# A second level of Strassen's scheme in four of the seven products of Q, K and V

## The chip, the core and the metric

The kernel runs on one core of one Trainium2 chip. The core has a matrix engine (TensorE, PE in the profile; its weight loads are the row PEld), a vector engine (VectorE, DVE), a scalar engine (ScalarE, ACT), a general engine (GpSimd, POOL) and a queue that issues most transfers (SyncE, SP). Each engine works through its own list of instructions in order and waits at semaphores for the others. The metric is device time in microseconds of one execution; the time shown is the median of three runs.

## The reference, cut to what matters

```python
x = L0_attn_a_x                                   # 8 x 512 x 1024, fp32
x = x + _L0_attn_a_ref(_layernorm(x), qkvw, qkvb, ow, ob)
x = x + _L0_ffn_ref(_layernorm(x), weight, bias, centroids, assignments)
x = x + _L0_attn_b_ref(_layernorm(x), bv_q, bv_k, bv_v)
x = x + _L0_ffn_ref(_layernorm(x), weight, bias, centroids, assignments)

def _L0_attn_a_ref(x, attn_qkvw, attn_qkvb, attn_ow, attn_ob):   # 32 heads of 32
    qkv = x @ attn_qkvw + attn_qkvb
    ...
    scores = jnp.einsum('bhqd,bhkd->bhqk', q, k) * scale
    probs = jax.nn.softmax(scores, axis=-1)
    ctx = jnp.einsum('bhqk,bhkd->bhqd', probs, v)
    return ctx @ attn_ow + attn_ob
```

The change concerns the first attention alone: the product `x @ attn_qkvw` (4096 x 1024 by 1024 x 3072) and how its result and the context are kept.

## The kernel before

All work is fp32. The program has four stages one after the other: softmax attention (some 2490 of 3715 us), a gated dense layer, a sigmoid attention, and the dense layer again. The instruction order on each engine is the order in which the Python code records it.

**Units.** The softmax attention runs over `units = 64` units: 8 batches of 512 tokens by `NC = 8` groups of four heads (128 columns of Q, K and V). Unit n is batch n // 8, group n % 8. In its turn unit n does the scores, exponentials and values of its own heads, while the row maxima of unit n + 1 and the projections of unit n + 2 are made beside it.

**The loop over a unit** (`for n in range(units)`, with `for i in range(TPB)` inside, four quarters). Each quarter records, in this order: `rows_step(n + 1, i)`, a block of scores (TensorE, L905) into the four PSUM banks `sc`, and its row maxima `nmax` by one reduction (VectorE, L906); a piece of side work and of the *filler* (`between`); `keys_step(n, i)`, which writes the same four banks again, first with the maxima as a shift (L934), then with the scores (L937), and ScalarE's exponential of them (L939); then more filler. `sum_step` adds the four exponential blocks (one addition by GpSimd in two halves, L948, two by VectorE, L950), `values_step` multiplies them with V (L961), `normalize` divides by the sum (L973 to L982) and writes the context `ctxT`. Quarter 0 also has `turn_max`, a small transposition (`tpm`) that takes its PSUM buffer from the same ring of three (`ps_m`, tag "mm") as all projections.

**The filler** is a queue of TensorE pieces of about 0.9 us each: the projections of unit n + 2 (`project_pieces`) and the out products of an earlier batch (`out_products`, shared over the units by `OUT_SHARES` and `LAST_SHARES`), woven into each other. `between` takes its share of the queue (`FILLER_SHARES`). Side work (`side`) is what VectorE, SP and GpSimd do for later batches: normalizing x (`norm_tasks`), the sums of the left matrices (`left_tasks`), of the weights (`sum_weights`) and of the out weights (`ow_sum_tasks`).

**Projections.** For batch 0 (units 0 to 7) they are plain products (`first_pieces`). From unit 8 on they follow Strassen's scheme in Winograd's form: seven products instead of eight, from sums of the left matrix (`LEFT`: A11, S2, A12, S3, A22, S1, S4) and of the right (`RIGHT`: B11, T2, B21, T3, T4, T1, B22). The left matrix is the normalized x, split in two halves of tokens and two halves of the 1024 inputs. The right matrix of Q and K is one unit's Q columns beside its K columns; that of V is the columns of two units. Each product has 256 tokens, 512 inputs and 128 columns and is gathered into the outputs by VectorE additions straight from PSUM (`gather`, with two ScalarE copies for the first product): L156 and L158. The T sums of the weights are made once in batch 0 and kept in DRAM; a `Stream` of blocks of 256 KB (`W_BUFS = 6` buffers) brings them back for each unit, in the order of `order`. The matmul itself is in `product` (L578), which splits a product by columns into matmuls of width 64 or 32.

**Context and out products.** The context of a whole batch is one tile `ctxT` (two of them in turn, 16 KB per partition each); its out products (again seven instead of eight per pair of token tiles) run during the next batch.

Of the kernel before, what the change touches and what calls it, by code (L numbers as in the profile page):

```python
# [13 lines left out]
F32 = mybir.dt.float32  # L14
# [3 lines left out]
ALU = mybir.AluOpType  # L18
# [19 lines left out]
W_BUFS, OW_BUFS = 6, 6  # L38
FILLER_SHARES = (0.5, 0.5, 0.6, 1.0, 1.0, 1.0, 0.7, 1.0, 1.0)

OUT_SHARES = (2, 2, 2, 1)

OUT_SUMS = {0: (0,), 5: (1, 2), 7: (3,)}
LAST_SHARES = {-7: 0, -6: 1, -5: 1, -4: 2, -3: 2, -2: 6, -1: 2}
# [103 lines left out]

def gather(nc, k, acc, ia, ib, ja, jb, bias=(None, None), early=False):
# [49 lines left out]
class Stream:  # L199
# [6 lines left out]
    def fill(self, upto):  # L206
        while self.loaded < min(upto, len(self.sources)):
            k = self.loaded
            self.tiles[k] = self.pool.tile(self.shape, F32, tag=self.tag, name=f"{self.tag}_{k}")
            self.nc.sync.dma_start(self.tiles[k], self.sources[k]())  # L210
            self.loaded += 1
# [209 lines left out]
def softmax_attention(tc, cst, stage, filler, clusters, pools, dr, late, args):  # L421
# [14 lines left out]
    fixed, ctxp, rpool, npool = outer("a_fixed", 1), outer("a_ctx", 2), outer("a_r", 3), outer("a_n", 1)  # L436
    owpool, csp, xTp, sump = outer("a_ow", OW_BUFS), outer("a_cs", 1), inner("a_xT", 2), inner("a_sum", 1)
    wpool, xpool = inner("a_w", W_BUFS), inner("a_x", 2)
    qkpool, vpool, ptp, tmp = inner("a_qk", 3), inner("a_v", 5), inner("a_pt", 3), inner("a_tmp", 1)
# [9 lines left out]
    xTs, ctxTs, state, lefts = {}, {}, {}, {}  # L449
    units, half = B * NC, NC // 2  # L450

    def quarter(t, g, k):

        return w_view[:, ts(k, half), ts(t * NC + g, P)]

    def weight_source(kind, g, name):

        if name[0] == "T":
            return dr.sums[kind, g, name].rearrange("p (c n) -> p c n", c=half)
        t, g = ((0, g) if name[2] == "1" else (1, g)) if kind == "qk" else (2, 2 * g + int(name[2]) - 1)  # L460
        return quarter(t, g, int(name[1]) - 1)

    V_PARTS = (RIGHT[:4], RIGHT[4:])
    order = []
    for u in range(NC, units):
        g = u % NC
        order += [("qk", g, RIGHT[k]) for k in EARLY] + [("v", g // 2, name) for name in V_PARTS[g % 2]]
# [11 lines left out]
    used, side, tiles, waiting, ready, held = {"w": 0}, deque(), deque(), deque(), deque(), []  # L479

    def first_norm():
# [5 lines left out]
        def load(i):  # L487
            pool, tag = (npool, ("n1", "nT")[i % 2]) if i > 1 else (xpool, "x")
# [31 lines left out]
    def norm_tasks(b):  # L520
# [9 lines left out]
        def load(i):  # L530
            st[i] = xpool.tile([P, H], F32, tag="x", name=f"x_{b}_{i}")
            nc.sync.dma_start(st[i], x[ts(b * TPB + i, P), :])
# [23 lines left out]
        def apply(k, j):  # L556
# [5 lines left out]
            [partial(load, 0), partial(load, 1)],  # L562
            [partial(turned, k) for k in range(NC // 2)] + [partial(stats, 0), partial(stats, 1)],
            [partial(load, 2), partial(load, 3)],
            [idle] * 3 + [partial(stats, 2), partial(stats, 3)],
            [root, shift, send, idle, spread],
            [idle, idle, *scaled[:3]],
            [idle, idle, *scaled[3:6]],
            [idle, idle, *scaled[6:]],
# [10 lines left out]
    first_w = {}  # L580

    def load_first(g, kinds):

        if g >= NC:
            return
        if not first_w:
            first_w["qk"] = ctxp.tile([P, NC, S], F32, tag="ctxT", name="w_first")
        if 2 in kinds:
            wv = rpool.tile([P, H], F32, tag="r", name=f"wv_{g}")
        for t in kinds:  # L590
            for k in range(2):
                at = ts(k, S) if t == 2 else ts((g % 2) * 4 + 2 * t + k, S)
                flat = wv if t == 2 else first_w["qk"].rearrange("p c t -> p (c t)")
                w = first_w[t, g, k] = flat[:, at].rearrange("p (c n) -> p c n", c=half)
                nc.sync.dma_start(w, quarter(t, g, k))
# [1129 lines left out]
```

## Time and profile before

| what | value |
|---|---|
| median of three runs | 3717.14 us (3715.69 to 3718.55) |
| span of the profiled execution | 3715.1 us |
| instructions | 76365 |
| GpSimd busy | 594.9 us, 16% |
| mean granted TensorE clock | 0.999 |
| bytes moved, mean rate | 598.55 MB, 161 GB/s |
| L906, reduction of scores, VectorE, x256 | 586.0 us, 2289 ns each |
| L950, sums of exponentials, VectorE, x128 | 292.0 us, 2281 ns each |
| L158, gather with bias, 128x256, x224 | 107.6 us, 480 ns each |
| L156, gather, 128x256 (v and qk), x196 and x168 | 79.8 and 70.0 us, 419 and 417 ns each |
| L578, matmuls of Q and K after batch 0 (128x256) | 408.5, 202.0, 119.2 and 19.5 us |
| L578, matmuls of V after batch 0 (128x128) | 198.4, 162.5 and 19.7 us |

How to read it: "busy" is the time in which an engine executes; a line like `128*64 128x256 f32 x16` is a group of 16 matmuls that contract 128 rows, use 64 columns of the array and move 256 columns. Each fp32 matmul of the program shows as two records. In brackets at the end of a timeline row stands how long the engine was idle before it and what ended that. Between the span and the median lie 2 us.

### The profile page before, as it was taken

How to read it: one execution, taken by the hardware profiler on the slowest of the kernel's cores; microseconds unless marked ns; L12 is line 12 of the kernel's file. 1: busy time of each engine (PE TensorE's matmuls, PEld its weight loads, DVE VectorE, ACT ScalarE, POOL GpSimd, SP SyncE). 2: the span in 40 equal slices, each digit the busy share in tenths (PEclk: the TensorE clock that was granted, in tenths of full speed). 3: DMA queues.
4: the chain of work that ended last, by engine and by line, in shares of the span. 5: the costliest groups of instructions: out<-in, count | busy, mean ns of one | idle time of the engine just before them, and what ended most of it. 6: DMA issues, size and time to landing. Idle time of an engine off the chain costs nothing.

```text
span 3715.1 us, 76365 instructions
## 1 busy us (share of the span) xinstructions
PE 3677.4 (99%) x32792; PEld 1876.7 (51%) x32792; DVE 2539.7 (68%) x3497; ACT 927.8 (25%) x1017; POOL 594.9 (16%) x574
## 2 busy tenths in 40 slices
PE   8999999999999999999999999999999999999999
PEld 4444544544545455445445445444444467774444
DVE  4777676767667677766767767666788845556656
ACT  1222222222222222222222222222111144430000
POOL 1222111111111111111111111111000044530000
PEclk9999999999999999999999999999999999999999
DMA  5335444645655555465465454347566767763332
GB/s 184 113 122 179 142 143 147 192 138 157 185 153 150 159 162 163 133 198 152 139 182 159 143 150 124 122 156 244 158 180 179 184 186 234 222 220 127 133 132 98
DMA packets 728641, 598.55 MB, mean 161 GB/s; under 512 B 322152, under 2 KB 574064, under 8 KB 728304
## 3 DMA queue, kind: packets, MB, share of 16 engines
q1 hardware_dynamic: 701072, 496.40, 46.6%
q0 software_dynamic: 22912, 81.54, 5.7%
q10 hardware_dynamic: 4320, 15.73, 1.0%
q8 instruction: 259, 4.24, 0.5%
q14 instruction: 78, 0.64, 0.0%
HBM read 459.30 MB, written 134.25 MB: 160 GB/s over the span
## 4 chain that ended last, share of the span: by engine, by line
PE 95%; DVE 3%; DMA 1%; issue 1%; ACT 0%; POOL 0%; SPq 0%; DVEq 0%; ACTq 0%; POOLq 0%
PE mm L578 42%; PE dense L1285 20%; PE sc L905 7%; PE av L961 6%; PE sc L937 6%; PE csc L1347 4%; PE o L1366 4%; PE sc L934 2%; PE logitsT L339 1%; PE den L973 1%; PE tp L291 1%; DVE nmax L906 1%; DVE sum L950 1%; PE tpm L578 0%; DVE s L1377 0%
## 5 line engine op out<-in xcount | busy, mean ns | idle before, releaser
L906 DVE TENSOR_REDUCE nmax<-sc 128x4 f32<-128x2048 f32 x256 | 586.0, 2289 | 295.3 <-PE sc L905 295.2
L939 ACT ACTIVATE pT<-sc 128x2048 f32<-128x2048 f32 x256 | 480.8, 1878 | 1122.3 <-PE sc L937 1122.3
L948 POOL TENSOR_TENSOR sum<-pT,pT 128x1024 f32<-128x1024 f32 x128 | 309.4, 2438 | 750.0 <-ACT pT L939 678.1
L578 PE MATMUL mm<-xT,w 128*64 128x256 f32 (+1 forms) x3736 | 428.1, 383 | 0.0
L578 PEld LDWEIGHTS mm<-xT,w 128*64 128x64 f32 (+1 forms) x3736 | 241.5, 135 | 204.1 <-issue 54.3
L578 PE MATMUL mm<-s,w 128*32 128x256 f32 (+1 forms) x3672 | 321.2, 381 | 1.2 <-DVE qk L158 1.2
L950 DVE TENSOR_TENSOR sum<-sum,pT 128x2048 f32<-128x2048 f32 x128 | 292.0, 2281 | 0.9 <-ACT pT L939 0.9
L905 PE MATMUL sc<-qk,qk 32*64 32x512 f32 x4096 | 285.1, 613 | 0.5 <-ACT pT L939 0.4
L156 DVE TENSOR_TENSOR u<-dense,u 128x512 f32<-128x512 f32 x223 | 148.0, 685 | 184.7 <-PE dense L1285 169.3
L578 PEld LDWEIGHTS mm<-s,w 128*32 128x32 f32 (+1 forms) x3672 | 180.4, 122 | 180.4 <-issue 68.9
L937 PE MATMUL sc<-qk,qk 32*128 32x512 f32 x2048 | 263.7, 589 | 0.0
L578 PE MATMUL mm<-ow,ctxT 128*32 128x512 f32 (+2 forms) x1276 | 247.2, 599 | 3.0 <-DMA ow<-o_T 2.8
L961 PE MATMUL av<-pT,v 128*32 128x512 f32 x2048 | 246.4, 598 | 0.2 <-ACT pT L939 0.2
L1285 PE MATMUL dense<-sum,s 128*128 128x512 f32 x512 | 231.8, 593 | 0.0
L578 PEld LDWEIGHTS mm<-w,xT 128*64 128x64 f32 (+1 forms) x3888 | 197.5, 133 | 62.2 <-issue 48.9
L578 PE MATMUL mm<-w,xT 128*64 128x128 f32 (+1 forms) x3888 | 218.1, 274 | 0.0
L158 DVE SCALAR_TENSOR_TENSOR qk<-mm,qkvb_s,qk 128x256 f32<-128x256 f32 x224 | 107.6, 480 | 123.2 <-PE mm L578 119.2
L1285 PE MATMUL dense<-wT_s,dT_b 128*128 128x512 f32 x384 | 171.2, 593 | 0.0
L1285 PE MATMUL dense<-wT_s,dT_a 128*128 128x512 f32 x384 | 171.2, 593 | 0.0
L578 PE MATMUL mm<-ow,c 128*64 128x512 f32 (+2 forms) x864 | 169.9, 596 | 0.2 <-DMA ow<-in_ow 0.2
L578 PE MATMUL mm<-w,s 128*64 128x128 f32 x2688 | 162.5, 274 | 0.0
L578 PEld LDWEIGHTS mm<-w,s 128*64 128x64 f32 x2688 | 148.0, 137 | 22.9 <-issue 22.9
(236 smaller groups left out, 4468.8 us busy)
## 6 DMA issues: line engine op xcount, KB each, us to landing
w<-in_qkvw SPq DMA_DIRECT2D x252, 256.0 KB, 3.0
ow<-o_T SPq DMA_DIRECT2D x240, 256.0 KB, 3.6
w<-qk_T SPq DMA_DIRECT2D x224, 256.0 KB, 2.8
ow<-in_ow SPq DMA_DIRECT2D x180, 256.0 KB, 3.3
w<-v_T SPq DMA_DIRECT2D x112, 256.0 KB, 2.7
x<-in_x SPq DMA_DIRECT2D x32, 512.0 KB, 5.3
dT_a<-xT SPq DMA_DIRECT2D x32, 512.0 KB, 5.7
x_a<-x SPq DMA_DIRECT2D x32, 512.0 KB, 6.5
```

What stands on the lines that cost most here:

```text
L156: nc.vector.tensor_tensor(out, acc, other, ALU.add)
L578: nc.tensor.matmul(out[cols], lhsT[:, cols], rhs, **flags)
L905: nc.tensor.matmul(sc[ts(j, P // 2), h, :], st["q"][rows, cols], st["k"][rows, :], start=True, stop=True)
L906: nc.vector.tensor_reduce(st["nmax"][:, qt, :], sc, AX.X, ALU.max, negate=True)
L937: nc.tensor.matmul(sc[:, h, :], st["k"][rows, ts(kt, P)], st["q"][rows, :], start=False, stop=True)
L939: nc.scalar.activation(pT, sc, AF.Exp, scale=SCALE_A)
L948: nc.gpsimd.tensor_tensor(st["sum"][:, h, :], st["pT", 0][:, h, :], st["pT", 1][:, h, :], ALU.add)
L950: nc.vector.tensor_tensor(st["sum"], st["sum"], st["pT", kt], ALU.add)
L961: nc.tensor.matmul(st["av"][rows, :], st["v"][:, kt, rows], pT[:, h, :], start=(kt == 0), stop=(kt == TPB - 1))
L1285: nc.tensor.matmul(st["acc"], st["left"][LEFT[k]][:, c, :], self.w[RIGHT[k]][:, c, :], start=(c == 0), stop=(c == half - 1),)
L1347: nc.tensor.matmul(sc[:, AT_OFF[i] : AT_OFF[i] + n], k[:, c, ts(i, P)], xT[:, c, i * P :], start=(c == 0), stop=(c == 1),)
L1366: nc.tensor.matmul(acc[:, j - jj, :], at[:, start : start + P], self.v[b * TPB + i][:, cols], start=(i == 0), stop=(i == j),)
```

## The change

Of the seven products of Q, K and V, four (S2, A22 and A12, S3 with their right sides) are made by a second Strassen step; the other three (A11 by B11, S1 by T1, S4 by B22) stay as they are. The four are taken in two pairs (`TWICE = ((2, 4), (1, 3))`): the inner products of a pair are summed in one PSUM accumulator of 128x2x128, so that a pair costs seven accumulators with four 128-column products each.

- Projections come in jobs: Q and K for two units (`("qk", n, part)`, two parts, one per unit of the loop), V for four units (`("v", n, part)`, four parts). `parts_of(u)` says which parts unit u carries in its filler.
- Each inner product is gathered by the same seven additions and two copies as an outer one; the three outer products are added by `done`, for two halves of the columns each.
- `left_tasks` makes the inner left sums too, in two portions in groups 4 and 5 of the batch before; `weight_sums` makes the inner weight sums in batch 0 and stores them with GpSimd's queue in `dr.twice` and `dr.once`, spread by `SUM_STEPS`.
- The weight stream now covers batch 0 as well and reads 20 blocks per job.
- The context is kept in six quarter slots (`ctx_s`, `SLOTS`), the last one in a spare tile that `settle` copies at the end of the loop.
- The rows of x for the layer norm are loaded into the place of the later `xT`, earlier than before; `qk` tiles go from 3 to 5, `v` from 5 to 7, out weight buffers from 6 to 5; the out products are shared otherwise.

```diff
-W_BUFS, OW_BUFS = 6, 6
+W_BUFS, OW_BUFS = 6, 5
+QK_BUFS, V_BUFS, SLOTS = 5, 7, 6
+SUM_STEPS = (16, 16, 16, 16, 10, 10, 10, 10, 9)
-OUT_SHARES = (2, 2, 2, 1)
+OUT_SHARES = (1, 2, 2, 2)
-LAST_SHARES = {-7: 0, -6: 1, -5: 1, -4: 2, -3: 2, -2: 6, -1: 2}
+LAST_SHARES = {-7: 0, -6: 0, -5: 1, -4: 2, -3: 4, -2: 4, -1: 3}
+TWICE = ((2, 4), (1, 3))
+STORED = ("B11", "T3", "B21", "B22", "T1", "T2", "T4")
...
+    def parts_of(u):
+        parts = [("first", u + 2, 0)] if u + 2 < NC else []
+        n = u + 3 if u % 2 else u + 2
+        if NC <= n < units:
+            parts.append(("qk", n, 0 if u % 2 else 1))
+        n = u - u % half + half
+        if NC <= n < units:
+            parts.append(("v", n, u % half))
+        return parts
+    def blocks_of(kind, n, part):
...
+        nodes = {"qk": ((0, 1), (2, 3, 4)), "v": ((0,), (1,), (2, 3), (4,))}[kind][part]
...
+        def twice(i, k, at):
+            def go():
+                assert i in left["made"]
+                acc, w = ps_m.tile([P, 2, P], F32, tag="mm", name="mm"), weights.tiles[at]
+                w = w.rearrange("p (a c) n -> p a c n", a=2)
+                for a in range(2):
+                    for c in range(2):
+                        lhsT, rhs = w[:, a, c, :], left[TWICE[i][a]][k][:, c, :]
+                        if not qk:
+                            lhsT, rhs = rhs, lhsT
+                        product(acc[:, a, :], lhsT, rhs, start=(c == 0), stop=(c == 1))
+                if k == 0:
+                    make(i)
+                o = [target(i, j) for j in range(2)]
+                gather(nc, k, acc, *(o[j][:, :, m, :] for m in range(2) for j in range(2)), early=True)
+                weights.done(at)
...
+        def done(node, j, acc):
+            (ia, ja), (ib, jb) = ([target(side, j)[:, m] for m in range(2)] for side in range(2))
+            qb, kb = (bias(side, j) if qk else None for side in range(2))
+            if node == 0:
+                add(ia, acc, qb)
+                add(ib, acc)
+                add(jb, ib)
+                add(ja, jb, qb)
+            elif node == 5:
+                add(jb, acc, kb)
+                add(ib, acc)
+            else:
+                add(ib, acc, kb)
...
+        steps = [
+            partial(tt, e1, b21, b22, ALU.add), partial(tt, e2, e1, b11, ALU.subtract),
+            partial(tt, e3, b11, b21, ALU.subtract), partial(tt, e4, b12, e2, ALU.subtract),
+        ]
+        steps.append(partial(last, 0))
+        steps += [partial(tt, a21, a11, a21, ALU.subtract), partial(tt, s2, a22, a21, ALU.subtract)]
+        more = [partial(tt, s4, a12, s2, ALU.subtract), partial(tt, s1, s2, a11, ALU.add)]
+        for node, t in ((1, s2), (3, a21)):
+            q11, q12, q21, q22 = quarters(t)
+            e = againp.tile([P, 3, 2, P], F32, tag=f"e{node}", name=f"e{node}_{b}")
+            names, own = left_sums(nc, q11, q12, q21, q22, *(e[:, k] for k in range(3)))
+            left[node] = [names[name] for name in LEFT]
+            more += own
+        more.append(partial(last, 1))
+        return steps, [partial(together, more[a:b]) for a, b in ((0, 1), (1, 6), (6, 11))]
...
+    def settle():
+        kept = ctxs[B - 1, 1]
+        first, second = sorted(free_slots[:2])
+        del free_slots[:2]
+        ctxs[B - 1, 1] = ctx_s[:, first : second + 1 : second - first]
+        for m in range(2):
+            nc.scalar.copy(ctxs[B - 1, 1][:, m], kept[:, m])
...
-            if g == NC - 2:
-                side.extendleft(reversed(left_tasks(b + 1)))
-            filler.add(weave(project_pieces(ahead), products), mark=ahead)
+        if b + 1 < B and g in (half, half + 1):
+            if g == half:
+                left_steps = deque(left_tasks(b + 1))
+            side.extendleft(reversed(left_steps.popleft()))
+        pieces = [piece for part in parts_of(n) for piece in job_pieces(*part)]
...
-    nc = bacc.Bacc("TRN2", target_bir_lowering=False, num_devices=1)
+    nc = bacc.Bacc("TRN2", target_bir_lowering=False, num_devices=1, dynamic_dma_scratch_size=4096)
```

## The prediction

> **What bounds the kernel now.** I read the page's busy line first, then the chain of waits, then one whole batch of the attention loop in the windows view, then the few places where TensorE waits at all.
>
> ```profile
> span 3715.1 us, 76365 instructions
> ...
> PE 3677.4 (99%) x32792; PEld 1876.7 (51%) x32792; DVE 2539.7 (68%) x3497; ACT 927.8 (25%) x1017; POOL 594.9 (16%) x574
> ...
> PE 95%; DVE 3%; DMA 1%; issue 1%; ACT 0%; POOL 0%; SPq 0%; DVEq 0%; ACTq 0%; POOLq 0%
> ```
>
> TensorE is never idle for long (38 us in all), so any matmul taken away shortens the run, as long as nobody else becomes late. One steady batch of the loop (eight units, from 1011.1 to 1328.8 us) shows who could:
>
> ```profile
> 1011.10:1328.80 317.70, 317.39 (x3734) 160.17 (x3733) 226.02 (x304) 84.43 (x83) 44.22 (x25) 1.00 0.54 160
> ```
>
> The columns are length, PE, PEld, DVE, ACT, POOL, clock, DMA share and GB/s. VectorE has 317.7 - 226.0 = 91.7 us free per batch. But it works in order, and each score block L905 must be reduced (nmax, L906) before the next block can be written (L934) into the same four PSUM banks. The one place in the loop where VectorE had too much to do shows the price; first TensorE, then VectorE, in order of time:
>
> ```profile
> 287.49 1.11 PE L905 MATMUL sc<-qk,qk 32*64 32x512 f32 x16
> 288.53 1.08 PE L578 MATMUL mm<-s,w 128*64 128x256 f32 x8
> 289.44 1.90 PE L578 MATMUL mm<-xT,w 128*64 128x256 f32 x16
> 293.64 0.41 PE L934 MATMUL sc<-shift,ones_h 32*128 32x512 bf16 x4 [2.30 <-DVE nmax L906]
> ```
>
> ```profile
> 278.86 2.29 DVE L906 TENSOR_REDUCE nmax<-sc 128x4 f32<-128x2048 f32 x1 [0.73 <-PE sc L905]
> 281.06 2.28 DVE L950 TENSOR_TENSOR sum<-sum,pT 128x2048 f32<-128x2048 f32 x1
> 283.26 1.22 DVE L1377 TENSOR_TENSOR s<-xT 128x1024 f32<-128x1024 f32 x1
> ...
> 291.31 2.28 DVE L906 TENSOR_REDUCE nmax<-sc 128x4 f32<-128x2048 f32 x1
> ```
>
> Between two reductions VectorE had 12.45 us of work, TensorE between the score blocks only 9.6. The second reduction started late and TensorE stood 2.30 us. In all, waits of this kind are few:
>
> ```profile
> PE sc L934 <- DVE nmax L906: 4.7, 5, 2.3
> ...
> PE tpm L578 <- DVE parts L916: 1.3, 2, 1.0
> ```
>
> So the kernel is bound by TensorE, with VectorE behind it at a small distance, in quarters of a unit.
>
> **The change, part by part. TensorE.** The six groups of L578 that make Q, K and V after the first batch have 408.5 + 202.0 + 119.2 + 19.5 us (128x256) and 198.4 + 162.5 + 19.7 us (128x128), less a little of other work: about 1130 us. Four of seven products cost 7/8 afterwards: 1/14 less, 81 us at most. I counted it again through the instruction lists of both kernels as built, cut at each score block, with prices from undisturbed stretches of the timeline: a full 128x128 product of 256 columns 0.451 us (1028.44 to 1032.05: eight products), of 128 columns 0.219 (1004.46 to 1006.21: eight), at width 32 0.46 and 0.2475. From the first to the last score block this gives 2423.5 us before and 2348.5 after. The tail of out products left behind grows by 1.0. TensorE: -74 us. The lists show that the change does what it says (84 groups of four 128-column products in each later batch), so that rival is dropped.
>
> [...] The rows show 2 x 0.219 = 0.438 against 0.451, no loss, and I keep 74.
>
> **VectorE.** Per batch the lists have 52 additions of 128x256 out of PSUM before and 136 after, besides 32 scalar_tensor_tensors in both: each inner product needs its own seven additions, then the outer sums 14 more per job. 84 x 0.417 (L156, v and qk) = 35.0 us. Left sums: four of 512 and eight of 256 more, 4 x 0.69 + 8 x 0.417 = 6.1. So +41 us per batch, 226 to 267 us, while TensorE falls from 317.7 to about 307 (the row sums of units 24 to 31 are 313.0 and 302.6). Additions from SBUF to SBUF at 128x256 are not in the trace; the nearest row (L1158, 256 wide) has 0.402, L156 has 0.417; I take 0.417. ScalarE's copies stay 24 per batch at 0.375.
>
> On average that still fits; by quarter it doesn't. Back to back, an operation takes its time less 0.08 us (the reduction 2.29, the next starts after 2.20), and 0.12 more where it needs the one before. Units 24 to 31 (all steady batches are alike), first and last quarter, TensorE / VectorE in us:
>
> | unit | 24 | 25 | 26 | 27 | 28 | 29 | 30 | 31 |
> |---|---|---|---|---|---|---|---|---|
> | first, before | 10.5/9.2 | 11.4/9.2 | 12.3/7.7 | 10.5/10.0 | 10.5/9.2 | 11.4/9.2 | 12.3/11.2 | 10.5/7.5 |
> | first, after | 10.5/12.8 | 11.4/10.7 | 11.4/11.0 | 10.5/12.7 | 10.5/15.1 | 11.4/14.6 | 11.4/11.0 | 10.5/13.0 |
> | last, before | 8.4/8.0 | 8.4/10.3 | 9.2/6.6 | 8.4/10.4 | 8.4/7.9 | 8.4/9.0 | 9.2/6.6 | 8.4/9.0 |
> | last, after | 8.4/8.3 | 8.4/9.5 | 8.6/12.7 | 8.5/8.4 | 8.4/9.6 | 8.4/8.3 | 8.6/11.4 | 8.5/8.0 |
>
> The 15.1 of unit 28, as an example: reduction 2.2, sum of exponentials 2.2, four inner left sums 2.5, two groups of four outer additions 3.4, statistics 1.6, normalizing 2.4, two more additions 0.8. The cover is the filler between a score block and its L934, less 2.35 for the reduction: 3.6 - 2.35 = 1.25, or 0.35 to 0.45 where the filler is 2.7 to 2.8. What VectorE has over TensorE is carried on, and TensorE stands for what exceeds the cover. Unit 28: 15.1 - 10.5 - 1.25 = 3.3. Unit 29: 1.2 carried + 3.2 - 0.4 = 4.0. Unit 27: 4.1 carried from the eight additions at once in unit 26 - 1.4 = 2.8, then 1.35 + 2.2 - 1.25 = 2.2. Unit 31: 1.5 and 2.6 likewise. Unit 24: 1.0. The middle quarters give nothing. Sum 17.4 us per batch.
>
> Over all units: 19.0 in the first batch (weight sums there), 18.7 in the second, 84.4 in the five after it, 9.4 in the last, 131.5 in all. The same count on the kernel before gives 9.6, against 6.0 measured in the two rows above; in the quarter shown it has 12.73 for 12.45. I take 2% off VectorE's times for that: 115 after, 6 before. VectorE: +109 us. Bounds: 4% off and 0.6 us more cover give 79; the raw count 131.5. Behind a standing L934 stand the exponentials (L939), the next score block and everything else in TensorE's order; nothing overtakes.
>
> **Transfers.** Weight blocks after the first batch grow from 588 to 840 of 256 KB, 36 more per batch, 9.4 MB in 307 us: 160 to about 191 GB/s. The page has slices of 234 and 244 GB/s without TensorE waiting, and a block lands 2.9 us after its issue; with six buffers five inner blocks of 4 x 0.219 = 0.88 us cover 4.4 us. I take 0; the ring of ow falls from six to five (5 x 0.9 = 4.5 us against 3.6), and ow waits were 2.8 us before; upper bound 20. The rows of x for the next batch now come four at once and earlier, into the place of the later xT: the same eight transfers on SP, whose queue stands 1524 us behind L578 already (SPq L210); 0. GpSimd issues 108 stores instead of 48 in the first batch at 0.54 + 0.18 us, 43 us beside its 15 to 25% busy there; 0, at worst eight groups of four in front of the sums of exponentials: 8 x 2.9 = 23. **End of the loop:** two copies of 1024 elements by ScalarE stand between the last normalizing and the out products; by its 128x512 rows (0.69) between 1 and 3 us; I take 2.
>
> **Sum:** 3715.1 - 74 + 109 + 2 = 3752 us span. The median is 2 us above the profiled span, so 3754.
>
> **Rivals.** (1) VectorE stays hidden: the additions take slack that really exists (68% busy), and the run falls by the whole TensorE term: 3717 - 74 + 2 = 3645. For it speaks the average, 267 of 307 us; against it the stop of 2.30 us at an excess of 2.85. It decides if fewer than 10 us of stops show on L934. 6%. (2) Stops, but half: if the additions run at 0.34 back to back even in chains and the cover is 0.6 longer, the count with 8% off is 54: 3717 - 74 + 52 + 2 = 3697, faster. Against it the agreement in the steady quarters (11.17 counted, 11.15 measured in unit 30). It turns to slower when stops exceed 80 us. 15%. (3) Weight and ow rings run dry or GpSimd's stores hold VectorE's sums as well: another 20 + 23 on top, about 3797. 7%.
>
> **How the numbers follow.** The forecast case, VectorE's queue takes more than TensorE gives back, holds 72%: 3722 (stops 79) to 3771 (131.5, less 6). The range 3690 to 3800 takes in (2) and (3) and leaves out (1). 0.2% is 7.4 us, about what a measurement of this kernel can tell. Faster: (1) and most of (2), 0.20; the same: the low end of the forecast and the high end of (2), 0.08; slower 0.72.
>
> **What would show it.** Right: L578's Q, K, V groups lose some 75 us; VectorE's busy time grows by about 320 us (7 x 41, and 40 of weight sums: twelve groups of 4 x 0.69 + 8 x 0.417 = 73 after, 48 x 0.69 = 33 before); the row "sc <- DVE nmax" grows from 4.7 to about 100 us, most of it in units 24, 27, 28, 29 and 31 and their like; the span of a steady batch is 307 + 17 = 324 instead of 317.7. Wrong: that row under 40 us, or waits for w or ow above 20, or TensorE's busy time not lower.

## The result, and the profile after

The changed kernel takes 3982.28 us (median of 4 runs, 3977.65 to 3983.76), the kernel before beside it 3716.41 (4 runs): 1.0712 times as long, 95% interval 1.0697 to 1.0728. The forecast was 3754. The direction was right, the size was not: 266 us more instead of 37.

From the page of the kernel after, span, busy time by engine, and the shares of the chain of waits:

```profile
span 3975.9 us, 80821 instructions
...
PE 3687.1 (93%) x34128; PEld 1930.6 (49%) x34128; DVE 2838.2 (71%) x4265; ACT 944.1 (24%) x1047; POOL 647.8 (16%) x634
...
PE 65%; DVE 20%; DMA 6%; issue 5%; SPq 2%; POOL 1%; ACT 0%; DVEq 0%; POOLq 0%; ACTq 0%
```

TensorE has less to do and yet is busy 10 us longer (3677.4 before). Idle it is for 289 us instead of 38. Both are seen in the windows view: batch 0 before, then batch 0 and one steady batch after, each from its first reduction to the first of the next batch (columns: length, busy PE, PEld, DVE, ACT, POOL, clock, DMA share, GB/s):

```profile
42.58:317.00 274.42, 271.47 (x2840) 122.59 (x2842) 186.89 (x204) 70.85 (x58) 62.77 (x67) 0.99 0.39 124
```

```profile
40.24:434.96 394.72, 313.72 (x3288) 152.09 (x3288) 260.18 (x364) 73.19 (x65) 115.73 (x127) 0.91 0.61 183
...
1093.30:1437.68 344.38, 316.07 (x3888) 167.62 (x3888) 260.04 (x394) 86.52 (x87) 43.96 (x25) 0.97 0.58 174
```

Length less busy PE is the idle time: 81 us in batch 0 and 28 in the steady batch, against 3 and 0.3. And the clock is new: 0.91 and 0.97. In the clock's records of the whole run TensorE is at half speed for 182 us, in 38 stretches (8 us in 3 stretches before). A stretch often begins while TensorE still stands, and idle time is not lost twice: busy it is for 135 of the 182 us (6.8 before), and half of that, 64 us more than before, is what the clock cost. What remains of the busy time without that half is the work at full speed: 3674.0 us before and 3619.5 after. So 251 us more idle + 64 of clock - 54 of work = 261, the difference of the two spans. The work is a remainder here, but a steady one: 307.6 to 307.8 us in each of batches 2 to 6 (315.0 to 315.2 before), whatever the clock did there. By stage, before and after (us; half clock is time spent at 0.5, and how much of it TensorE was busy; batch 7 ends at the first reduction of its last unit):

| stage | length | idle | half clock | busy at half clock |
|---|---|---|---|---|
| start | 42.6 to 40.2 | 12.2 to 11.1 | 0 to 3.4 | 0 to 3.4 |
| batch 0 | 274.4 to 394.7 | 2.9 to 81.0 | 3.4 to 71.7 | 3.4 to 38.9 |
| batch 1 | 304.4 to 317.1 | 1.5 to 20.3 | 0 to 10.2 | 0 to 10.1 |
| batches 2 to 6, each | 315.4 to 342.7 | 0.3 to 27.4 | 0 to 17.8 | 0 to 15.3 |
| batch 7 | 263.6 to 251.3 | 1.6 to 14.4 | 0 | 0 |
| rest | 1253.0 to 1259.1 | 18.0 to 25.2 | 4.5 to 8.0 | 3.4 to 6.2 |

Not all of the 120 us by which batch 0 is longer is loss: 24 us are work that the new order does there instead of later (batches 1 and 7 have 11 and 25 us less). Idle time and clock cost it 96 us.

What ended TensorE's waits, over the whole run after (us in all, times, longest):

```profile
PE sc L1091 <- DVE nmax L1063: 97.7, 54, 14.8
PE tpm L629 <- DVE parts L1073: 42.5, 19, 8.5
PE den L1157 <- DVE qk L164: 34.1, 16, 3.6
PE mm L629 <- DMA w<-t_v: 33.2, 14, 5.0
PE mm L629 <- DVE qk L164: 12.7, 13, 6.7
PE mm L629 <- DMA ow<-o_T: 11.0, 11, 2.4
```

The first row is the wait that the prediction was about (L934 <- nmax there). It met its "about 100" by luck: 40 us of it lie in batch 0, and VectorE's lateness shows as well at two places that the prediction left out: the turning of the maxima (tpm) and the sums for the normalizing (den). Weight blocks and out weights late together: 44 us.

How the clock comes in is seen on TensorE's timeline after (start, duration, instruction, idle time before it):

```profile
1171.41 1.09 PE L629 MATMUL mm<-w,xT 128*64 128x128 f32 x16
1172.59 1.09 PE L629 MATMUL mm<-w,e 128*64 128x128 f32 x16
1178.49 1.97 PE L629 MATMUL mm<-w,e 128*64 128x128 f32 x16 [4.80 <-DMA w<-t_v]
1180.39 2.01 PE L1062 MATMUL sc<-qk,qk 32*64 32x512 f32 x16
```

A stop of 4.80 us for a weight block, and then the same sixteen matmuls take 1.97 us instead of 1.09. In the trace of after 21 of 21 stops of 3 us or more are followed by such a stretch within 7.5 us, 16 of 25 between 2 and 3 us, and 7 of 38 between 1 and 2.

### The profile page after: what moved, and what is told of

The parts are those of the page before. It is cut to its first block, busy times and chain, and to the rows that moved or that the text cites. A ratio compares the mean times of both kernels' runs of the same rounds, so it can differ in the third digit from the quotient of the medians.

```text
span 3975.9 us, 80821 instructions
## 1 busy us (share of the span) xinstructions
PE 3687.1 (93%) x34128; PEld 1930.6 (49%) x34128; DVE 2838.2 (71%) x4265; ACT 944.1 (24%) x1047; POOL 647.8 (16%) x634
## 4 chain that ended last, share of the span: by engine, by line
PE 65%; DVE 20%; DMA 6%; issue 5%; SPq 2%; POOL 1%; ACT 0%; DVEq 0%; POOLq 0%; ACTq 0%
PE mm L629 23%; PE dense L1476 19%; DVE nmax L1063 5%; PE av L1118 4%; PE sc L1062 4%; PE sc L1094 4%; PE o L1557 3%; PE csc L1538 3%; DVE sum L1107 3%; DMA w<-t_v 2%; DMA ow<-o_T 2%; DVE v L831 2%; PE sc L1091 1%; PE logitsT L350 1%; DVE ln_st L252 1%
## 5 line engine op out<-in xcount | busy, mean ns | idle before, releaser
L629 PE MATMUL mm<-xT,w 128*64 128x128 f32 (+6 forms) x4160 | 397.3, 351 | 2.9 <-DVE qk L164 2.9
L629 PEld LDWEIGHTS mm<-xT,w 128*64 128x64 f32 (+2 forms) x4160 | 232.4, 136 | 176.5 <-issue 95.8
L1062 PE MATMUL sc<-qk,qk 32*64 32x512 f32 x4096 | 290.4, 623 | 11.5 <-DVE nmax L1063 10.1
L629 PE MATMUL mm<-s,w 128*64 128x256 f32 (+3 forms) x3104 | 287.2, 355 | 11.5 <-DVE qk L164 9.8
L164 DVE TENSOR_TENSOR u<-dense,u 128x512 f32<-128x512 f32 x223 | 148.0, 685 | 184.9 <-PE dense L1476 169.5
L1094 PE MATMUL sc<-qk,qk 32*128 32x512 f32 x2048 | 274.4, 609 | 0.0
L629 PE MATMUL mm<-ow,ctx_s 128*64 128x512 f32 (+2 forms) x1076 | 247.7, 601 | 19.4 <-DMA ow<-o_T 9.8
L629 PEld LDWEIGHTS mm<-s,w 128*64 128x64 f32 (+1 forms) x3104 | 176.1, 132 | 153.6 <-issue 51.3
L164 DVE TENSOR_TENSOR qk<-mm,qk 128x256 f32<-128x256 f32 x392 | 157.6, 419 | 96.0 <-PE mm L629 79.6
L629 PE MATMUL mm<-e,w 128*64 128x128 f32 (+1 forms) x4048 | 204.5, 279 | 1.1 <-ACT lg_a L361 1.1
L629 PEld LDWEIGHTS mm<-e,w 128*64 128x64 f32 (+1 forms) x4048 | 178.2, 128 | 56.0 <-issue 19.3
L629 PE MATMUL mm<-w,xT 128*64 128x128 f32 (+4 forms) x2632 | 193.4, 296 | 3.2 <-DVE v L164 3.2
L1091 PE MATMUL sc<-shift,ones_h 32*128 32x512 bf16 x1024 | 103.4, 392 | 98.2 <-DVE nmax L1063 97.7
L629 PE MATMUL mm<-ow,c 128*32 128x512 f32 (+2 forms) x1004 | 171.9, 597 | 1.4 <-DMA ow<-o_T 1.2
```

The lines of the kernel that those rows point to most:

```text
L164: nc.vector.tensor_tensor(out, acc, other, ALU.add)
L629: nc.tensor.matmul(out[cols], lhsT[:, cols], rhs, **flags)
L1062: nc.tensor.matmul(sc[ts(j, P // 2), h, :], st["q"][rows, cols], st["k"][rows, :], start=True, stop=True)
L1091: nc.tensor.matmul(sc[:, h, :], cst.ones_h[rows, :], st["shift"][rows, :], start=True, stop=False)
L1094: nc.tensor.matmul(sc[:, h, :], st["k"][rows, ts(kt, P)], st["q"][rows, :], start=False, stop=True)
```

## The experiments

All times are medians; the ratio is to the kernel before in the same job (3714 to 3715).

| kernel | us | ratio, 95% interval |
|---|---|---|
| before, more VectorE (more_dve) | 3741.4 | 1.0071 (1.0056 to 1.0086) |
| before, short stops (stop_short) | 3766.0 | 1.0138 (1.0117 to 1.0158) |
| before, long stops (stop_long) | 3915.3 | 1.0539 (1.0518 to 1.0560) |
| after, loads early (ahead) | 3929.6 | 1.0577 (1.0561 to 1.0593) |
| after, tiles turned by TensorE (turn_pe) | 3968.0 | 1.0680 (1.0664 to 1.0696) |
| after, fewer additions (no_inner) | 3929.5 | 1.0580 (1.0563 to 1.0598) |
| after, writes from ScalarE's queue (send_act) | 4021.2 | 1.0821 (1.0802 to 1.0839) |
| after, loads replaced (no_loads) | 3986.0 | 1.0726 (1.0710 to 1.0742) |
| ahead, norm steps apart (apart) | 3932.8 | 1.0591 (1.0575 to 1.0607) |
| ahead, rebalanced with GpSimd (rebalanced) | 3952.7 | 1.0637 (1.0622 to 1.0653) |
| ahead, other layout (layout) | 3950.7 | 1.0629 (1.0611 to 1.0647) |
| layout, tiles turned by TensorE (layout_turn) | 3906.5 | 1.0517 (1.0501 to 1.0533) |
| layout_turn, V first (layout_v) | 3905.6 | 1.0517 (1.0500 to 1.0535) |
| layout_turn, no sum on GpSimd (no_hold) | 3873.8 | 1.0423 (1.0400 to 1.0445) |

### Is it the additions? (more_dve, no_inner)

```diff
+        for _ in range((0, 1, 1, 1, 1, 2, 1)[k]):
+            extra = tmp.tile([P, S], F32, tag="rden", name="extra")
+            nc.vector.tensor_tensor(extra[:, : 2 * P], acc, other, ALU.add)
```

> The kernel before with as many additions more on VectorE as the inner products bring (84 of 128x256 per batch from batch 1 on, 35 us, each behind a product of Q, K and V and reading its accumulator), into a spare tile; TensorE's work is the same. Total theory (the additions are what stops TensorE): 17 us of stops and 5 of clock per batch, 3717 + 7 x 22 = about 3870. Quarter theory: by the tally the old order of work has room, 35 us of stops instead of 6, with the clock 3750 to 3765.

Measured 3741.4, 27 us more than before and 9 below the quarter theory's range. VectorE is nearly as busy in a steady batch as after the change (253.9 of 319.6 us, 260.0 of 344.4), but TensorE's idle time grows from 0.3 to 4.2 us only, in stops of at most 1.7 us, and the clock stays whole:

```profile
945.96:1265.58 319.62, 315.44 (x3708) 159.37 (x3706) 253.94 (x382) 85.07 (x83) 44.05 (x25) 1.00 0.54 158
```

So the amount of additions is not what costs 266 us; in the old order of work there is room for them.

```diff
+                if k in (0, 3, 4):
                     gather(nc, k, acc, *(o[j][:, :, m, :] for m in range(2) for j in range(2)), early=True)
```

> The changed kernel without five of the seven gathering additions of each set of inner products (two are kept, which write a tile first): 60 additions of 128x256 fewer per batch, 25 us of VectorE, 267 to 242 per steady batch. Part of Q, K and V is left out by it. If the additions alone make VectorE's stops (total theory): VectorE's 17.6 us of stops per steady batch vanish, with the clock some 22 per batch, about 3820 to 3850. If what counts is what VectorE has in single quarters, inner left sums and bunched outer additions too (quarter theory): the tally falls from 115 to 80 only, 35 us, with the clock about 50: 3930.

Measured 3929.5, where the quarter theory said 3930 and the total theory 3820 to 3850. With 25 us less on VectorE a steady batch still has 20.8 us of idle time and a clock of 0.98:

```profile
1077.84:1410.37 332.53, 311.72 (x3888) 164.21 (x3888) 237.35 (x334) 86.45 (x87) 43.76 (x25) 0.98 0.62 180
```

The nearness to 3930 is partly luck: of the 52 us between the two profiled spans 43 are idle time, 4 clock and 4 work, where the expectation had 35 us of stops and 15 of clock.

### What a stop costs (stop_short, stop_long)

```diff
+        acc = ps_m.tile([P, P], F32, tag="mm", name="held")
+        nc.tensor.matmul(acc, cst.ident_h, cst.ident_h, start=True, stop=True)
+        for _ in range(copies):
+            nc.scalar.copy(acc, acc)
+        nc.tensor.matmul(acc, cst.ident_h, cst.ident_h, start=True, stop=True)
...
+            if i == 2 and NC <= n < units - NC:
+                held_up(2)
```

> The kernel before with one short stop of TensorE in each of 48 units (batches 1 to 6), behind the third score block: a small product, two copies of it by ScalarE in its accumulator (128x128), and a product over it that must wait. By ScalarE's 0.375 us for 128x256 a stop is some 0.8 to 1.3 us. Clock theory (a stop from about 2 to 2.5 us on is followed by 3.4 us at half clock, a shorter one by nothing): time grows by the stops alone, 40 to 62 us, 3757 to 3779, and no time at half clock is added. If any stop costs clock: 3840 to 3860.

> The same with ten copies instead of two, stops of 2.4 to 3.5 us at the same 48 places. Clock theory: 48 x 3.4 = 164 us at half clock, so 82 us beyond the stops themselves (115 to 170): 3915 to 3970. If the clock has nothing to do with the stops: the stops alone, 3832 to 3887, and no time at half clock.

The stops came out at 0.7 us (31.8 in all) and 2.9 us; the second in the view of the waits, and one of them on TensorE's timeline:

```profile
PE held L1002 <- ACT held L1001: 139.9, 48, 3.0
```

```profile
410.52 0.22 PE L1002 MATMUL held<-ident_h 128*128 128x128 bf16 x1 [2.87 <-ACT held L1001]
410.67 5.36 PE L578 MATMUL mm<-s,w 128*64 128x256 f32 x32
```

Thirty-two matmuls, 3.8 us at full clock (sixteen of this shape take 1.90 in the kernel before), take 5.36: 1.6 more, about half of 3.4. With the short stops time grows by 51.3 us: 31.8 of stops and 19.5 for the 96 small products and what hangs on them, which the expectation had left out; time at half clock does not grow (3.6 us). With the long ones it grows by 200.5: 139.9, the same 19.5, and 41 more, against 107 us at half clock in 29 stretches (8 in 3 before). By the profiled spans the three are 140.2 of idle time, 16.4 of work and 46.4 of clock, half of the time busy at half speed. The work at full speed comes out alike with short and with long stops, 3691.3 and 3690.4 us, so that this way of pricing the clock holds.

Only 27 of the 48 stops were followed by half clock, not all as expected. Why these, the traces settle: all stretches begin on one grid of 3.413 us (within 5 ns), in this run and in after, and what counts is how far a stop empties one window of that grid. Of the 48 stops 24 left a window in which TensorE was busy for less than 40%: all were followed by half clock. Nine were divided by the grid so that both windows stayed over 50% busy: none was. Of the 15 between, 3 were. In the traces of before, after and the 14 experiments together (windows at full clock, from 15 us on) half clock followed 333 of 333 windows under 40%, 55 of 181 between 40 and 50%, and 0 of 17125 above. So stops of 2.9 us were enough in 27 of 48 cases, and a window did not have to be idle for it: in after seven windows were 34 to 40% busy, and half clock followed all seven.

### Batch 0: work or waiting? (ahead, apart, no_loads)

VectorE's timeline in batch 0 of after shows what stood at the head of its queue:

```profile
98.39 0.69 DVE L651 TENSOR_TENSOR wy_qk<-wx_qk,wy_qk 128x512 f32<-128x512 f32 x1 [6.41 <-DMA wx_qk<-in_qkvw]
...
123.01 0.69 DVE L651 TENSOR_TENSOR wy_qk<-wx_qk,wy_qk 128x512 f32<-128x512 f32 x1 [5.64 <-DMA wx_qk<-in_qkvw]
...
159.95 3.62 DVE L610 TENSOR_TENSOR xT<-xT,rows 128x1024 f32<-128x1024 f32 x3 [13.85 <-DMA rows<-rows]
```

The loads were late because SyncE's queue stood for the buffers, whose stores had not landed (after, 40 to 400 us):

```profile
SPq L644 <- DMA t_qk<-wx_qk: 68.2, 7, 15.4
SPq L644 <- DMA t_v<-wx_v: 39.4, 4, 15.2
```

```diff
-            xs = [npool.tile([P, H], F32, tag=tag, name=f"wx_{kind}_{job}_{c}") for tag in ("n1", "nT")]
+            if even:
+                xs = [npool.tile([P, H], F32, tag=tag, name=f"wx_{kind}_{job}_{c}") for tag in ("n1", "nT")]
+            else:
+                xs = [ctx_s[:, slot].rearrange("p c t -> p (c t)") for slot in (4, 5)]
...
-    sums = deque(step for job in jobs for c in range(2) for step in weight_sums(*job, c))
+    made = [weight_sums(*job, c, c == 0) for job in jobs for c in range(2)]
+    sums = deque([made[0][0], made[1][0], lambda: None])
+    for m, (_, steps) in enumerate(made):
+        if 0 < m < len(made) - 1:
+            steps.insert(3, made[m + 1][0])
+        sums.extend(steps)
```

> The changed kernel; only the loads for the weight sums of batch 0 come one portion earlier, each second portion into the two context slots that batch 0 leaves empty, so that VectorE and SyncE's queue need not stand for a load or a store. Sums, stores and products are the same, 12 portions of eight additions. Theory W (too much work on VectorE per quarter): the tally of stops changes by 1.5 us, so 3960 to 3985 us, and TensorE still stands some 80 us in batch 0. Theory D (VectorE had nothing to do but stood at the head of its queue for data): TensorE's idle time in batch 0 falls from 81 to 20 to 30 us and its time at half clock from 72 to 15 to 25 us, together 75 to 85 us less: about 3900.

Measured 3929.6, 53 us less than after; by the profiles 49 of it lie in batch 0 (394.7 to 345.3): idle time 42 instead of 81, half clock 31 instead of 72. The work is the same, so about half of the 96 us that batch 0 lost was waiting for transfers. It is less than theory D said; a stop of 13.8 us for the norm's rows stayed.

```diff
-            for _ in range(2 if len(norms) > half - n else 1):
-                side.extend(norms.popleft())
+            apart = [step for _ in range(2 if n in (0, 2) else 1) for step in norms.popleft()]
...
+            for j, step in enumerate(apart):
+                upto = len(steps) * (j + 1) // (len(apart) + 1)
+                side.extend(steps[at:upto] + [step])
+                at = upto
```

> The kernel with the early loads (3929.6), and in batch 0 the layer norm's steps for batch 1 spread evenly between the weight sums, so that the pass over xT does not come to the head of VectorE's queue before its rows have landed. TensorE's and VectorE's work is the same; the tally of stops rises by 4 us. Theory D: the stops of 13.8 and 2.2 us in unit 1, with 6.8 us of clock behind them, go: 3905 to 3915. If the first batch's stops come from VectorE's amount of work: 3930 to 3940.

Measured 3932.8: no gain. The stop in unit 1 shrank to 4.0 us and one of 14.2 came up in unit 0.

```diff
-                nc.sync.dma_start(dst, src.rearrange("(k c p) n -> c p k n", k=2, c=2)[c])
+                nc.scalar.copy(dst, ob_s[:, : 4 * P].rearrange("p (k n) -> p k n", k=2))
```

> The changed kernel, the loads for the weight sums of batch 0 replaced by copies that ScalarE makes of a tile that is there (48 of 128x512, 0.7 us each); sums and stores are as they were, their values are not the weights', so that four of the seven products of Q, K and V are left out in effect. Theory D (batch 0 waits for transfers and for SyncE's queue behind them): idle time of batch 0 from 81 to 25 us or less, near the tally's 17, half clock from 72 to 20: 3895 or less. Theory W (VectorE's work): idle time stays above 60, time within 25 us of 3982.

Measured 3986.0, as after. This kernel could not decide between the theories: it has no loads, but still what they had waited for. The copies stood in ScalarE's queue for the same stores, and the exponentials behind them:

```profile
ACT wx_qk L643 <- DMA t_qk<-wx_qk: 60.1, 6, 24.7
```

```profile
PE sc L1090 <- DVE nmax L1062: 79.5, 50, 16.0
PE sc L1061 <- ACT pT L1095: 44.0, 13, 10.2
```

It does show that the landing of the stores from buffers used again stops whichever queue holds the next writer: SyncE's for 108 us in after, ScalarE's here. That it, and not the landing of the loads, is the long part is likely by this, but not shown. How the last 40 us of idle time in batch 0 divide is not settled.

### Late weight blocks (turn_pe, send_act)

```diff
-        norm, logits = tiles.popleft()(blocks=wait)
+        norm, logits = tiles.popleft()(blocks=False)
```

> The changed kernel; the normalized tiles of the attention loop are turned by TensorE again, as after the loop, instead of being written to memory in 32x32 blocks by four transfers of SyncE's queue (row xT<-nB) and read back. That adds 43 us to TensorE by the row sums and takes 4.6 us per batch from VectorE. Theory W: the stops stay (the tally gives 123 instead of 115), so 3982 + 43 + 8 = about 4030. Theory D (weight blocks land late because the block writes fill the transfer engines and SyncE's queue): the stops on w (33 us, of which 6.0 per steady batch) and the half clock after them (6.8 us per steady batch, 3.4 lost) vanish, -50 to -65: 3965 to 3985.

```diff
-                self.nc.sync.dma_start(dst[i], blocks[ts(i, 32)].rearrange("q (c j t) -> q c j t", c=NC, j=n))
+                self.nc.scalar.dma_start(dst[i], blocks[ts(i, 32)].rearrange("q (c j t) -> q c j t", c=NC, j=n))
```

> The changed kernel with the four block writes of each normalized tile (xT<-nB) issued by ScalarE's queue instead of SyncE's; the bytes are the same. Queue theory (weight blocks are issued late behind these writes in SyncE's order): the waits on w and ow (33 and 11 us) fall below 10 together, with the clock behind them 50 to 65 us less: 3915 to 3935. Load theory (the transfer engines are full of small packets then, 300 to 430 GB/s): the waits stay, within 15 us of 3982.

With the tiles turned by TensorE: 3968.0, although TensorE has 32 us more work at full speed (43 by the row sums of the expectation). The waits on transfers, turn_pe's first and then those of send_act:

```profile
PE mm L629 <- DMA w<-t_v: 4.6, 4, 1.6
PE mm L629 <- DMA ow<-o_T: 4.1, 3, 2.1
```

```profile
PE mm L629 <- DMA w<-t_v: 40.9, 16, 4.8
PE mm L629 <- DMA ow<-o_T: 16.2, 9, 3.5
```

Moving the writes to another queue left the waits (and cost 28 us after the loop); taking them away, with the reading back, removed most of them. So the writes themselves are in the way, not their place in SyncE's order. How they are is open. In after, from 1160 to 1180 us, 4419 of 6473 packets are under 512 bytes, the engines move 300 to 430 GB/s from 1169 us on, and five blocks w<-t_qk take a median of 7.3 us to land, against 3.0 over the whole run. But without the writes, in turn_pe from 1150 to 1180 us, four such blocks took a median of 7.2. And the kernel before makes the same 96 writes and waits only 3 us for w and ow. So the writes alone are not enough; after the change there are also 36 weight blocks more per batch beside them.

### Laying the work out by quarters (rebalanced, layout, layout_turn, layout_v, no_hold)

```diff
+            engine = nc.vector if b == 1 else nc.gpsimd
+            engine.tensor_tensor(part, part, rows, (ALU.mult, ALU.add)[k])
...
-            nc.vector.tensor_tensor(r[m], r[m], ob_s, ALU.add)
+            nc.gpsimd.tensor_tensor(r[m], r[m], ob_s, ALU.add)
...
-            filler.add(weave(pieces, products), mark=n)
+            filler.add(weave(pieces, products, NC <= n < units - NC), mark=n)
...
-            between()
+            between(i > 0 or n >= NC)
```

> The kernel with the early loads (3929.6) and VectorE's work laid out by quarters: left sums except four, the bias of the residual and, from the third batch on, the layer norm's two passes over xT go to GpSimd; in the later batches a unit's out products come before its Q, K, V products; in batch 0 the layer norm's steps are spread between the weight sums and no side work runs in front of the first quarter's filler, and more weight sums fall in unit 5. TensorE's work is the same. By the tally VectorE's stops fall from 114 to 25 us, from 15.3 to 1.1 per steady batch. Quarter theory: 3930 - 90, less some 35 of clock, less 15 to 25 for the wait on the layer norm's rows in batch 0: about 3785 (3755 to 3815), with the waits on w and ow (52 us) left. If what counts is not where the work lies, or if GpSimd's work now holds VectorE: above 3860.

Measured 3952.7, slower than the kernel it was made from. The waits put down to VectorE did fall, from 172 to 118 us, but two other kinds of stop came up. One is seen on VectorE's timeline, GpSimd's and TensorE's beside it:

```profile
1283.45 0.41 DVE L836 TENSOR_TENSOR qk<-mm,qk 128x256 f32<-128x256 f32 x1
1283.90 10.02 DVE L836 TENSOR_TENSOR qk<-qk 128x256 f32<-128x256 f32 x1
1293.96 2.44 DVE L838 SCALAR_TENSOR_TENSOR qk<-qk,qkvb_s,qk 128x256 f32<-128x256 f32 x1
```

```profile
1284.30 2.38 POOL L929 TENSOR_TENSOR r<-r,ob_s 128x1024 f32<-128x1024 f32 x1
1286.62 4.73 POOL L1110 TENSOR_TENSOR sum<-pT,pT 128x1024 f32<-128x1024 f32 x2
1291.31 2.33 POOL L1181 TENSOR_TENSOR xT<-xT 128x1024 f32<-128x1024 f32 x1
```

```profile
1298.36 1.12 PE L630 MATMUL mm<-s,w 128*64 128x256 f32 x4 [7.98 <-issue]
```

An addition of 0.42 us lasts 10.02 while GpSimd adds, and TensorE stands until VectorE has come to the accumulators behind it; six stops of 8 us like this one make 48 us (the profile names no releaser for them). In the attention stage 68 of VectorE's operations last over one and a half times the shortest of their kind and 0.15 us more: they are held, 164 us in all; none of them reads an accumulator in PSUM. The other is that the out products put together ran ahead of their ring: waits on ow grew from 15.5 to 58.8 us, the longest 11.6.

```diff
+            filler.add(weave(pieces, products, NC <= n < units - NC and g > 0), mark=n)
```

> The last one, and the work laid out otherwise, all of it staying on VectorE: out products before Q, K, V products in seven of eight units, no side work in front of the first quarter's filler in batch 0, more weight sums in unit 5. This is the rebalanced kernel without what went to GpSimd. Tally of VectorE's stops 70 us instead of 118, steady batch 8.7 instead of 15.3. Quarter theory: 48 us less with some 20 of clock, from the run above (3910 expected): about 3840. If GpSimd was what spoiled the rebalanced kernel, no VectorE operation should take 10 us here, and the waits on nmax fall below 50 us; if the layout itself spoils it, the time stays above 3920 and waits on ow of 10 us appear.

> The same, and the tiles turned by TensorE instead of through memory: 43 us more for TensorE, stops on w and ow (52 us in the early loads kernel) below 10, with some 25 of clock. 14 us less came of it before: about 3825, the best that these parts together should give, and still slower than the kernel before (3715).

3950.7 and 3906.5, both far above the expectation; the tally of quarters failed here. In layout VectorE's waits stayed at 171 us, and a weight block came 12.3 us late in batch 0. No operation took 10 us, but 45 were still held in either kernel, because out products first had moved the two additions SBUF to SBUF behind each first outer product into the stretch where GpSimd sums exponentials (layout_turn):

```profile
1184.48 0.42 DVE L833 TENSOR_TENSOR qk<-qk 128x256 f32<-128x256 f32 x1
...
1186.35 2.08 DVE L833 TENSOR_TENSOR qk<-qk 128x256 f32<-128x256 f32 x1
1188.46 2.52 DVE L835 SCALAR_TENSOR_TENSOR qk<-qk,qkvb_s,qk 128x256 f32<-128x256 f32 x1
```

```profile
1185.73 4.97 POOL L1107 TENSOR_TENSOR sum<-pT,pT 128x1024 f32<-128x1024 f32 x2 [34.14 <-ACT pT L1098]
```

```diff
-            parts.append(("v", n, u % half))
+            parts.insert(len(parts) - (u % 2 == 0 and len(parts) > 0 and parts[-1][0] == "qk"), ("v", n, u % half))
```

> The layout_turn kernel with V's products ahead of Q's and K's in the even units, so that the additions from SBUF to SBUF behind the first outer product do not come while GpSimd sums two tiles of exponentials (in layout_turn 0.42 us became 2.08 and 2.52 then, 45 operations held, 75 us), and with the weight sums of batch 0 as in the early loads kernel (8 per unit from unit 4 on, not 12 and 18 in units 4 and 5, where SyncE's queue stood for their buffers and the weight blocks behind came 12.7 us late). Hold theory: fewer than 15 operations held, the waits on nmax fall from 90 to 40 us or less; the tally is 43 instead of 71. Batch 0 gives back some 25 to 35 us, the steady batches 10 each with the clock: 3906 - 100 = about 3805. If the holding costs TensorE nothing: only the tally's 28 and batch 0, about 3850, and the waits on nmax stay above 60.

Measured 3905.6: a miss. Now V's additions of the same kind met GpSimd's sum (41 held, 81 us), and batch 0 did not get faster (343 us). Hence the last run, which takes GpSimd's sum away.

```diff
-                nc.gpsimd.tensor_tensor(st["sum"][:, h, :], st["pT", 0][:, h, :], st["pT", 1][:, h, :], ALU.add)
+            nc.scalar.copy(st["sum"], st["pT", 0])
```

> The layout_turn kernel (3906.5) with GpSimd's addition of the first two tiles of exponentials replaced by ScalarE's copy of the first (128x2048, some 1.9 us), so that the second tile is left out of the sum. Hold theory: of the 45 held operations (75 us) nearly all are gone, the stops of 2.1 us on nmax in the third quarters of units 26 and 30 and their like vanish, 4 to 7 us per batch with the clock, 30 to 50 in all: 3855 to 3877. If holding costs TensorE nothing: within 10 us of 3906.

Measured 3873.8, 33 us less than layout_turn, in the hold theory's range: 1 operation of the stage held instead of 45, and of the steady batch's waits on nmax 7.3 us instead of 10.2, the two of 2.1 us gone. A steady batch has 17 us of idle time instead of 22. So being held does cost TensorE time, some 4 us per batch in this layout. In after itself ten operations of the stage are held, 19 us: it is no large part of the 266.

No version beat the kernel before. The best that computes everything, layout_v, is 5.2% slower.

## Why the prediction was right or wrong

- **TensorE -74: right in kind, 20 us too much.** The work at full speed fell by 54.5 us, in a steady batch from 315.2 to 307.6 where the row sums had 313.0 and 302.6. A product of 128 columns at width 64 was priced at 0.219 us from one stretch of eight; over the whole run, from start to start at full clock, it takes 0.229 before and 0.234 after, one of 256 columns 0.453. By the number of products that is some 10 of the 20 us, and the out products took 6 us more where 1 was counted. So two halves do cost more than the whole, 0.468 to 0.453, where the one stretch had 0.438 to 0.451. The projections lost 63 us, not 75.
- **VectorE's queue takes more than TensorE gives back: right in kind and place.** For the batches after the first the raw count was 112.5 us (131.5 less 19.0); waits ended by VectorE there are 55.3 (nmax) + 34.1 (den) + 24.3 (parts) + 8.6 + 6.0 + 3.4 = 131.7. For a steady batch, counted 17.4, the waits are 18.4: 7.3 + 4.9 + 3.2 and three small ones. They lie in the units of the table, 24, 27, 28, 29 and 31, and right behind 26 and 30, where the last quarter's lateness, which the table had too, meets the turning of the maxima. The 2% taken off VectorE's times made it worse, and the row L1091 alone was the wrong measure: where VectorE is late, TensorE stands at whatever it needs next. That crowded quarters make these stops rests on the count and on their places. Of the runs, more_dve and no_inner speak for it; the layouts took at most a part of the stops away, and the tally failed where it was used to foretell them.
- **"19.0 in the first batch (weight sums there)": the first step that failed.** 76.6 us of VectorE's waits lie there. The count took each addition to start when the one before ended. But the sums were put at the head of an in-order queue and waited for loads, these for single buffers, these for stores; and the norm's rows came 14 us late in the same queue. The prediction counted the transfers of this chain and priced them at nothing, because the queue "stands 1524 us behind L578 already": idle time of a queue was read as room, while what mattered was the landing time of its waits in a row. Early loads alone gave back 49 us of batch 0.
- **The price of a stop: the second, and the largest single term.** A microsecond of stop was counted as one. 64 us of the result are the clock after the stops, and no row of before was missing for it: behind the stop of 2.30 us shown there the eight matmuls of L937 took 1.90 us instead of 1.03, and the records have 3.4 us at half clock.
- **"Transfers. I take 0": the third.** 44 us of stops on w and ow instead of 3, beyond the upper bound of 20, with clock behind the longer ones. The cover of 4.4 us against 2.9 us of landing was compared with a median; in a crowded stretch a block took 7.3. The mean of 174 GB/s hid stretches of 430.
- **GpSimd's stores, 0: right for GpSimd (no wait of TensorE is ended by it that was not there before), wrong for the buffers** (above). The issues took 0.76 us each, 0.72 foretold.
- **The row "sc <- DVE nmax" near 100 and VectorE's busy time +320** came out at 97.7 (by luck, as said) and +298.5; the steady batch, foretold as 324, is 343. The condition set for "wrong" (waits for w or ow above 20, TensorE's busy time not lower) was met twice.
- **Rival (3)**, rings run dry and stores in the way, had a part of it right: the rings did run dry, for about 41 us more than before where it had 20. Its 23 us for GpSimd's stores in front of the sums of exponentials were not seen; that the total of 43 is near 41 is luck.
- **A slip in the bounds:** 3722 is a span and 3771 a median; the two differ by 2 us.

In all, each less what the kernel before had: 3717 - 54 + 128 (VectorE, later batches) + 74 (batch 0) + 41 (w, ow) + 64 (clock) = 3970, and 12 us elsewhere (7 of idle time behind the loop among them, not traced further).

## What to carry to other kernels

Where one engine bounds a kernel without a pause, a second engine's slack must be counted in the shortest stretch between two of their meetings, and a stop must be priced with the clock after it: here half clock followed none of the 17125 windows of 3.413 us that were more than half busy, and each window worked at half clock after one under 40% cost half of itself, 1.7 us (1.6 measured in stop_long). Work put into slack brings its waits along: before moving it to the head of an in-order queue, follow each operand back to the buffer that it needs and the store that frees it. And an engine that is 16% busy is not free to take more: beside GpSimd's additions in rebalanced one of VectorE's took 10.02 us instead of 0.42, and TensorE stood 8 us behind it.

## What the runs showed of the hardware

- Half clock after a stop came in pieces of 3.413 us or multiples (up to four, 13.7 us, in after), on one grid through a run. In 16 traces it followed every window of the grid in which TensorE was less than 40% busy (333) and none that was more than half busy (17125). Stops of 2.9 us brought it on in 27 of 48 cases, by where they fell in the grid; stops of 0.7 us in none.
- VectorE's additions with two operands in SBUF took longer beside GpSimd's: 0.42 us became 2.08 (layout_turn) and 10.02 (rebalanced, beside four additions of GpSimd), 0.48 with a bias became 2.52 and 2.44; without GpSimd's sum (no_hold) 1 operation of the stage was held instead of 45. Those that read PSUM kept their time: in after, 67 of L164 ran beside GpSimd's additions and none took over 0.43.
- With four 128 KB writes in 32x32 blocks per tile TensorE waited 44 us on w and ow in after, 57 with the writes on ScalarE's queue, and 9 without them (turn_pe), but 3 in the kernel before, which makes the same writes. That they lengthen the landing of a block is not shown: 7.3 us beside them, 7.2 in a like stretch without.
